# State-space stage of a three-part kernel: regrouping the matrix work by tile size

## The chip, the cores and the metric

The kernel runs on one core of a Trainium2 chip. The metric is the device time of one execution in microseconds (us). Engines go by the names of the profile: PE is TensorE (matmuls), PEld its weight loads, DVE is VectorE, ACT is ScalarE, POOL is GpSimd, SP is SyncE, which here only issues DMAs. All arithmetic is in 32-bit floats; the trace shows two PE instructions for each matmul of this type, and one for each transpose.

## What is computed

An image batch of 4 x 128 channels x 64 x 64 goes through three parts, each added to its input: convolutions with a non-local attention; a bidirectional state-space layer on the 4096 tokens of each image; a sigmoid recurrence over the tokens. The change touches only the second. For one direction it computes, with `A` negative and one `dt` for each token and head:

```python
zxbcdt = x @ in_proj
z, xbc, dt = jnp.split(zxbcdt, [D_INNER, D_INNER + CONV_DIM], axis=-1)
xbc = jax.nn.silu(conv)                      # 4 taps along the tokens
xh, Bm, Cm = jnp.split(xbc, [D_INNER, D_INNER + D_STATE], axis=-1)
...
Lmat = jnp.exp(_segsum(dAc.transpose(0, 1, 3, 2)))      # lower triangle, 0 elsewhere
Y_diag = jnp.einsum('bcln,bcsn,bchls,bcshp->bclhp', Cc, Bc, Lmat, xc)
states = jnp.einsum('bcln,bclh,bclhp->bchpn', Bc, decay_st, xc)
...
Y_off = jnp.einsum('bcln,bchpn,bclh->bclhp', Cc, prev, jnp.exp(Acs))
...
yg = y.reshape(b, l, D_INNER) * jax.nn.silu(z)
yn = yg * jax.lax.rsqrt(jnp.mean(yg * yg, -1, keepdims=True) + EPS) * norm_w
return yn @ out_proj
```

`_segsum` takes the differences of cumulated decays of two tokens of a chunk, and minus infinity where the second token is later. There are 4 heads of 64 channels, a state of 64, and both directions are summed. The result does not depend on the chunk length; the kernel uses 128.

## The kernel before

`mamba` (from L894) walks through 128 steps, 32 for each of the 4 images; a step is one chunk of 128 tokens in both directions. Four steps make a group of 512 tokens; `j` is the step within its group, `G` the group. The loop (L1415 to L1486) works on step n, prepares step n + 1 and loads step n + 2, and between these it does a part of the group's work for the next group (projections) and the last one (outputs), chosen by `j`.

A step's own work on PE, in its order, with the part of the array that each matmul uses (rows x columns):

- `states` (L1212): two products of `bt` and `xdtd` (128x64) into `p_st`. VectorE then adds them to the carried state S (L1230), which GpSimd has multiplied by the chunk's decay (L1227).
- `turn` (L1176): four transposes (128x128) of the next step's x into one PSUM bank.
- `scan` (L1233): eight products of `xdt` and `lt` (128x64, L1240) into `y`; then eight of the carried state S and `ct` (64x64, L1248).
- `prepare` (L1188), for the next step: one transpose of B into `p_bt` (128x128, L1193), two products of B and C into `p_g` (64x128, L1195). ScalarE takes the exponential of the whole of `lt` (L1197) and copies `p_bt` to `bt` (L1199). VectorE multiplies x by dt and dtd (L1202), `p_g` by a triangle of ones (`gm`, L1206), and `lt` by `gm` (L1207). GpSimd multiplies `ct` by C (L1208).

`p_g`, `p_bt` and `p_st` are parts of one PSUM tile, `small`, of two banks.

`lt` [128, 2 directions, 4 heads, 128] starts as a DMA (`load`, L1159) that spreads the row of cumulated decays over all partitions; it has three buffers. `differences` (L1169), at the end of step n for step n + 2, makes it relu(cs - row) on ScalarE, eight instructions with a bias for each partition; Relu keeps the exponent of the part that the triangle will cut from growing. `ct` is loaded in the same way and has two buffers.

The group's work by `j`, the PE part first: j=0 squares of the last group (ScalarE), `project` (L1124), `project_bc` (L1099), `project`; j=1 `means` (L1284, 128x32), `project`, `project_bc`; j=2 `project_fwd` (L1116), `activate`, four `project_z` (L1147), `gate` on GpSimd; j=3 `gate`, and the outputs of the last group in `back` (L1347). `project`, `project_fwd`, `project_z` and `outputs` use the whole array (128x128), `project_bc` uses 128x64, with the two directions in the two halves of the columns. All these take their PSUM tiles from `ring`, which has three banks. From step 4 of an image on, one piece of the next image's opening (`open_sequence`: statistics by transposes, then the scaled input, then the decays) is done at the end of each step, and at every odd step from 5 a piece of the closing statistics of the image before (`ended`).

PE and ScalarE run in the order in which the program is written (`manual_schedule`). VectorE, GpSimd and the DMA queue of SP are put into an order by the framework's planner, by program order and its own estimate of when things are ready[...].

## Time and profile before

| what | value |
|---|---|
| time, median of three runs | 3100.1 us (3091.95 to 3103.64) |
| the profiled execution | 3095.44 us, its span 3093.7 us |
| granted TensorE clock, mean | 0.973 |
| first part (convolution, attention) | to about 1640 us |
| state-space stage | about 1640 to 2960 us |
| busy in 1660 to 2920 us: PE / ACT / DVE / POOL | 1188 / 1019 / 887 / 724 us of 1260 |
| `lt` load, issue to landing | 5.5 us, 512 KB, 128 times |
| ScalarE table loads in lines L1197, L1113, L1122 | 88, 63 and 31 times, 1.28 us each |

The span runs from the first to the last instruction; the time of an execution has 1.7 us more around it. Matmuls are pipelined: the profile's busy time of one is longer than the distance to the next, so PE's cost is best read from start to start in the timeline. In a line of the timeline the first number is the start, the second the length, then engine, line, operation, output <- inputs, for a matmul the rows*columns of the array that it uses, and the shape. What stands in brackets at the end of a line is idle time before it and what ended it. In the list of waits the numbers are the sum in us, how often and the longest; in a group's row they are busy time and the mean of one in ns, then idle time before it.

### The profile page before, as it was taken

The page shows a single profiled execution, that of the slowest core. Times are in us where ns is not written, and L with a number is a line of the kernel's source. Part 1 is how long each engine was busy: PE and PEld are TensorE (multiplying, and loading weights), DVE is VectorE, ACT ScalarE, POOL GpSimd, SP SyncE. Part 2 cuts the span into 40 slices and gives each one's busy share as a digit, 9 for nine tenths or more (in the row PEclk, how much of TensorE's full clock was granted, in tenths as well). Part 3 has the DMA queues.
Part 4 walks back from the last instruction along what each step waited for, and adds up shares of the span by engine and source line. Part 5 has one row for each costly group of instructions (what it writes and reads, how often), then busy time and mean ns, then how long its engine had stood idle before and what let it go on. Part 6 is the DMA issues. An engine that isn't in the chain of part 4 may idle for free. (4 is left out here: it accounts for less than half of the span.)

```text
span 3093.7 us, 51126 instructions
## 1 busy us (share of the span) xinstructions
PE 2858.4 (92%) x19607; PEld 1461.9 (47%) x19607; DVE 2245.6 (73%) x3461; ACT 1834.4 (59%) x3134; POOL 1812.9 (59%) x1393
## 2 busy tenths in 40 slices
PE   6799999999999999999997999998999999999886
PEld 2345444454444554444463444444544444555455
DVE  6886677777787767788865767676777767676667
ACT  3253445444454444444526878876888778888756
POOL 4167458557585575876652565566556565555644
PEclk9899999999999999999998999999999999999988
DMA  5310011010100101011023343433333343333332
GB/s 185 136 39 31 24 47 34 21 44 24 47 32 23 44 24 47 28 50 44 16 81 92 90 124 86 109 88 113 96 96 92 91 103 97 100 102 101 83 111 111
DMA packets 108426, 224.68 MB, mean 73 GB/s; under 512 B 25678, under 2 KB 29390, under 8 KB 106764
## 3 DMA queue, kind: packets, MB, share of 16 engines
q1 hardware_dynamic: 96588, 177.53, 19.8%
q10 hardware_dynamic: 11584, 43.78, 4.2%
q8 instruction: 157, 2.57, 0.4%
q14 instruction: 97, 0.79, 0.1%
HBM read 200.83 MB, written 20.44 MB: 72 GB/s over the span
## 5 line engine op out<-in xcount | busy, mean ns | idle before, releaser
L480 DVE TENSOR_TENSOR es<-es,ex 128x1024 f32<-128x1024 f32 x448 | 703.0, 1569 | 83.6 <-ACT ex L463 43.2
L463 ACT ACTIVATE ex<-pf 128x1024 f32<-128x1024 f32 x512 | 497.8, 1021 | 403.8 <-PE pf L461 365.0
L461 PE MATMUL pf<-theta,phi 64*64 64x512 f32 x4096 | 496.7, 599 | 19.2 <-ACT ex L463 18.8
L473 PE MATMUL acc<-ex,gT 64*64 64x512 f32 x4096 | 486.7, 596 | 7.9 <-ACT ex L463 7.9
L1208 POOL TENSOR_TENSOR ct<-ct,Cst 128x512 f32<-128x512 f32 x128 | 170.0, 1328 | 344.0 <-DMA ct<-csmem 304.8
L1174 ACT ACTIVATE lt<-lt,cs 128x128 f32<-128x128 f32 x1024 | 312.1, 390 | 0.4 <-DMA lt<-csmem 0.4
L367 PE MATMUL pm<-yf,wt 128*128 128x256 f32 x1152 | 287.6, 382 | 15.9 <-DVE es L486 11.5
L473 PEld LDWEIGHTS acc<-ex,gT 64*64 64x64 f32 x4096 | 158.5, 135 | 298.2 <-issue 286.5
L461 PEld LDWEIGHTS pf<-theta,phi 64*64 64x64 f32 x4096 | 147.3, 133 | 311.7 <-issue 212.7
L367 PEld LDWEIGHTS pm<-yf,wt 128*128 128x128 f32 x1152 | 212.6, 189 | 99.2 <-issue 43.5
L410 ACT ACTIVATE eo<-pm 128x256 f32<-128x256 f32 x88 | 33.8, 384 | 367.6 <-PE pm L367 367.6
L1109 PE MATMUL pb<-tl,wbc_fwd 128*64 128x512 f32 x512 | 240.9, 614 | 6.9 <-DVE xT L1141 6.9
L1109 PE MATMUL pb<-tl,wbc_bwd 128*64 128x512 f32 x512 | 241.5, 615 | 0.0
L337 POOL TENSOR_TENSOR yf<-yd 128x272 f32<-128x272 f32 x192 | 230.4, 1228 | 1.4
L1273 POOL TENSOR_TENSOR yT<-yT,zT 128x512 f32<-128x512 f32 x127 | 170.9, 1351 | 57.2 <-DVE yT L1260 49.9
L1207 DVE TENSOR_TENSOR lt<-lt,gm 128x1024 f32<-128x1024 f32 x128 | 178.3, 1393 | 1.9
L337 POOL TENSOR_TENSOR yf<-xp 128x272 f32<-128x272 f32 x128 | 119.0, 961 | 97.4 <-PE pm L367 91.6
L1141 DVE SCALAR_TENSOR_TENSOR xT<-px,taps_bwd,xT 128x512 f32<-128x512 f32 x192 | 143.6, 748 | 9.7 <-ACT xT L1135 5.1
L1109 PEld LDWEIGHTS pb<-tl,wbc_fwd 128*64 128x64 f32 x512 | 66.6, 140 | 173.9 <-issue 142.1
L1240 PE MATMUL y<-lt,xdt 128*64 128x128 f32 x2048 | 141.2, 280 | 6.9 <-PE ptr L1183 4.2
L367 PE MATMUL pm<-yf,wc 128*128 128x256 f32 x512 | 133.4, 389 | 14.8 <-DVE eo L414 8.2
L1227 POOL TENSOR_TENSOR S<-S,tot 128x256 f32<-128x256 f32 x120 | 89.6, 746 | 96.1 <-PE y L1248 85.2
(299 smaller groups left out, 5714.9 us busy)
## 6 DMA issues: line engine op xcount, KB each, us to landing
lt<-csmem SPq DMA_DIRECT2D x128, 512.0 KB, 5.5
wt<-wd ACTq DMA_DIRECT2D x72, 576.0 KB, 3.7
ct<-csmem SPq DMA_DIRECT2D x256, 128.0 KB, 5.2
rs<-m SPq DMA_DIRECT2D x31, 512.0 KB, 3.7
wd<-t SPq DMA_DIRECT2D x16, 576.0 KB, 2.8
t<-in_x SPq DMA_DIRECT2D x4, 2048.0 KB, 10.7
rows<-after SPq DMA_DIRECT2D x32, 256.0 KB, 5.2
out<-t SPq DMA_DIRECT2D x4, 2048.0 KB, 14.3
```

The source lines that it names most:

```text
L337: nc.gpsimd.tensor_tensor(f[:, kx], at(x), at(y), op)
L367: nc.tensor.matmul(pm[:, e, :], wt, src, start=(i == 0), stop=(i == len(terms) - 1))
L461: nc.tensor.matmul(pf[c, e, :], phi[HALF[e], m, c], th[HALF[e]], start=True, stop=True)
L463: nc.scalar.activation(ex, pf, AF.Exp, scale=scale)
L473: nc.tensor.matmul(acc[r][HALF[e]], gT[HALF[r], 2 * m + e, :], ex[HALF[r], e, :], start=(m == 0), stop=(m == NT // 2 - 1),)
L480: nc.vector.tensor_tensor(es, es, ex, ALU.add)
L1109: nc.tensor.matmul(out, w[i]["bc"][:, tap, bass.ts(c, DS)], src, start=(tap == 0), stop=(tap == KC - 1),)
L1141: nc.vector.scalar_tensor_tensor(at(n), px, taps[:, PAD - n : KC - n], at(n), ALU.mult, ALU.add)
L1174: nc.scalar.activation(v, v, AF.Relu, scale=-1.0, bias=m["b"]["cs"][:, d, m["i"], h : h + 1])
L1207: nc.vector.tensor_tensor(lt, lt, gm.unsqueeze(2).to_broadcast([P, ND, NHEAD, P]), ALU.mult)
L1208: nc.gpsimd.tensor_tensor(m["ct"], m["ct"], Cs[:, cols].unsqueeze(1).to_broadcast([P, NHEAD, P]), ALU.mult)
L1273: eng.tensor_tensor(v, v, gr["z"][d][:, :, half(d, j // 2)], ALU.mult)
```

## The change

Five things are changed together.

1. Tile sizes. Products that used 128 columns of the array are issued as two products of 64 columns each (`product`), so `project`, `project_fwd`, `project_z` and `outputs` become 128x64; `means` goes from 128x32 to 128x64; the `p_g` products go from 64x128 to 64x64 (`likeness`). Transposes stay 128x128.
2. Order in a step. `scan` is split into `scan` (products with `lt`) and `carried` (products with S). The new order is `states`, `scan`, `turn` (which now includes the transpose of B), `tokens`, `carried`, `likeness`, `weigh`, then the group's work. `prepare` is dissolved: `tokens` has the copy of `p_bt` and the products with dt and dtd, `weigh` the products of `lt` and of `ct`. Pieces of the opening at steps 4 to 11 of an image, and all of the closing statistics, move from the end of the step to the place between `tokens` and `carried`.
3. Decays. The row and cs are stored negated. GpSimd writes 1e30 into the part of `lt` that the triangle would cut (`mask`, two selects a step), at the start of step n for step n + 2. At the end of step n ScalarE takes exp(bias - lt) in eight instructions (`decays`), instead of Relu there and one exponential in the next step. `gm` and the triangle product are gone; `lt` is multiplied by `p_g` from PSUM.
4. Buffers. `small` becomes two tiles of one bank: the first holds `p_g` of direction 0 and `p_bt`, the second `p_g` of direction 1 and `p_st`. `ct` has three buffers.
5. VectorE is added to the engines that run in program order.

```diff
-        engines = (mybir.EngineType.PE, mybir.EngineType.Activation)
+        engines = (mybir.EngineType.PE, mybir.EngineType.Activation, mybir.EngineType.DVE)
...
-        small = ps.tile([P, 2, NC], F32, name="small")
-        p_g, p_bt, p_st = small[:, :, 0:P], small[:, 0, P : 2 * P], small[:, 1, P : P + DI]
+        small = [ps.tile([P, NC], F32, name=f"small{d}") for d in range(ND)]
+        p_g, p_bt, p_st = [v[:, 0:P] for v in small], small[0][:, P : 2 * P], small[1][:, P : P + DI]
+
+        def product(out, w, src, start=True, stop=True):
+
+            for half in HALF:
+                nc.tensor.matmul(out[half], w[:, half], src, start=start, stop=stop)
...
-            nc.vector.tensor_copy(flat(cs), pcs[:, 0])
+            nc.vector.tensor_scalar(flat(cs), pcs[:, 0], -1.0, None, ALU.mult)
...
-            nc.scalar.activation(row[:, 1], pr, AF.Exp)
+            nc.scalar.activation(row[:, 1], pr, AF.Exp, scale=-1.0)
...
-            nc.tensor.matmul(px, wx, tl[:, rows(g, i, PAD)], start=True, stop=True)
+            product(px, wx, tl[:, rows(g, i, PAD)])
...
-            m["ct"] = wk.tile([P, NHEAD, P], F32, tag="ct", name="ct")
+            m["ct"] = wk.tile([P, NHEAD, P], F32, tag="ct", name="ct", bufs=3)
...
-        def differences(m):
+        def mask(m):
+
+            for d, step in enumerate((-1, 1)):
+                v = m["lt"][:, d]
+                nc.gpsimd.affine_select(
+                    out=v, in_=v, compare_op=ALU.is_ge, fill=1e30, base=0,
+                    pattern=[[0, NHEAD], [-step, P]], channel_multiplier=step,
+                )
+
+        def decays(m):
 
             for d in range(ND):
                 for h in range(NHEAD):
                     v = m["lt"][:, d, h, :]
-                    nc.scalar.activation(v, v, AF.Relu, scale=-1.0, bias=m["b"]["cs"][:, d, m["i"], h : h + 1])
+                    nc.scalar.activation(v, v, AF.Exp, scale=-1.0, bias=m["b"]["cs"][:, d, m["i"], h : h + 1])
...
+            nc.tensor.transpose(p_bt, gr["bc"][0][:, bass.ts(i % MT, P)], k.ident)
+
+        def likeness(m):
+
+            Bs, Cs = (m["g"]["bc"][c] for c in range(2))
+            at = m["i"] % MT * P
+            for h in range(2):
+                for d in range(ND):
+                    nc.tensor.matmul(
+                        p_g[d][HALF[h]], Bs[HALF[d], ds(at + h * DS, DS)], Cs[HALF[d], ds(at, P)],
+                        start=True, stop=True,
+                    )
+
+        def tokens(m):
+
             m["bt"] = wk.tile([P, P], F32, tag="bt", name="bt")
             nc.scalar.copy(m["bt"], p_bt)
...
-            gm = wk.tile([P, ND, P], F32, tag="gm", name="gm")
-            nc.vector.tensor_tensor(gm, p_g, k.tri, ALU.mult)
-            nc.vector.tensor_tensor(lt, lt, gm.unsqueeze(2).to_broadcast([P, ND, NHEAD, P]), ALU.mult)
...
+        def weigh(m):
+
+            for d in range(ND):
+                v = m["lt"][:, d]
+                nc.vector.tensor_tensor(v, v, p_g[d].unsqueeze(1).to_broadcast([P, NHEAD, P]), ALU.mult)
+            Cs = m["g"]["bc"][1][:, bass.ts(m["i"] % MT, P)]
+            nc.gpsimd.tensor_tensor(m["ct"], m["ct"], Cs.unsqueeze(1).to_broadcast([P, NHEAD, P]), ALU.mult)
...
             if n + 2 < N:
                 open_step(n + 2)
+                mask(m[n + 2])
             if n % NT == 0:
                 S = None
             S1 = states(m[n], S)
+            if n % 2 == 0:
+                y = ps.tile([P, ND, 2, 2 * P], F32, tag="y", name="y")
+            scan(m[n], y, S)
...
             if n + 1 < N:
                 turn(m[n + 1])
-            if n % 2 == 0:
-                y = ps.tile([P, ND, 2, 2 * P], F32, tag="y", name="y")
-            scan(m.pop(n), y, S)
+                tokens(m[n + 1])
+            turns = 4 <= at < 4 + NT // GT
+            if turns:
+                run(islice(opening, 1))
+            if at >= 5 and at % 2:
+                run(islice(ending, 1))
...
+            carried(m.pop(n), y, S)
             S = S1
             if n + 1 < N:
-                prepare(m[n + 1])
+                likeness(m[n + 1])
+                weigh(m[n + 1])
...
             if n + 2 < N:
-                differences(m[n + 2])
-
...
+                decays(m[n + 2])
+
+            if at >= 4 and not turns:
                 run(islice(opening, 1))
```

More of the change, by code (lines that the diff above doesn't have):

```diff
@@ L940, in mamba @@
         nc.gpsimd.memset(wdt, 0.0)
-        mean = wp.tile([P, QT], F32, name="mean")
+        mean = wp.tile([P, HD], F32, name="mean")
         nc.gpsimd.memset(mean, 0.0)
@@ L1084, in steps @@
             yield
-            pr = p_g if b == 0 else ring.tile([P, ND, P], F32, tag="big", name="pr")
+            pr = ring.tile([P, ND, P], F32, tag="big", name="pr")
             for i in range(ND):
@@ L1120, in project_fwd @@
             for tap in range(KC):
-                nc.tensor.matmul(px, w[0]["x"][:, tap, :], tl[:, rows(g, 0, tap)], start=(tap == 0), stop=(tap == KC - 1))
+                product(px, w[0]["x"][:, tap, :], tl[:, rows(g, 0, tap)], tap == 0, tap == KC - 1)
             nc.scalar.activation(gr["x"][0][:, 0, :], px, AF.Silu, bias=w[0]["cb"][:, 0:1])
@@ L1151, in project_z @@
             pz = ring.tile([P, MG], F32, tag="big", name="pz")
-            nc.tensor.matmul(pz, w[i]["z"][:, bass.ts(c, P)], tl[:, rows(g, i, PAD)], start=True, stop=True)
+            product(pz, w[i]["z"][:, bass.ts(c, P)], tl[:, rows(g, i, PAD)])
             nc.scalar.activation(gr["z"][i][:, c, :], pz, AF.Silu)
@@ L1186, in turn @@
                     )
-        def prepare(m):
-            gr, i = m["g"], m["i"]
-            Bs, Cs = gr["bc"][0], gr["bc"][1]
-            cols = bass.ts(i % MT, P)
-            nc.tensor.transpose(p_bt, Bs[:, cols], k.ident)
-            for d in range(ND):
-                nc.tensor.matmul(p_g[:, d, :], Bs[HALF[d], cols], Cs[HALF[d], cols], start=True, stop=True)
-            lt = m["lt"]
-            nc.scalar.activation(lt, lt, AF.Exp, scale=-1.0)
+            nc.tensor.transpose(p_bt, gr["bc"][0][:, bass.ts(i % MT, P)], k.ident)
[9 more added lines that the diff above has]
+        def tokens(m):
             m["bt"] = wk.tile([P, P], F32, tag="bt", name="bt")
@@ L1202, in prepare @@
                 nc.vector.tensor_tensor(
-                    m[name], m["xh"], m["b"][name][:, :, i, :].unsqueeze(3).to_broadcast([P, ND, NHEAD, HD]), ALU.mult
+                    m[name], m["xh"], m["b"][name][:, :, m["i"], :].unsqueeze(3).to_broadcast([P, ND, NHEAD, HD]), ALU.mult
                 )
-            gm = wk.tile([P, ND, P], F32, tag="gm", name="gm")
-            nc.vector.tensor_tensor(gm, p_g, k.tri, ALU.mult)
-            nc.vector.tensor_tensor(lt, lt, gm.unsqueeze(2).to_broadcast([P, ND, NHEAD, P]), ALU.mult)
-            nc.gpsimd.tensor_tensor(
-                m["ct"], m["ct"], Cs[:, cols].unsqueeze(1).to_broadcast([P, NHEAD, P]), ALU.mult
-            )
+        def weigh(m):
[4 more added lines that the diff above has]
+            nc.gpsimd.tensor_tensor(m["ct"], m["ct"], Cs.unsqueeze(1).to_broadcast([P, NHEAD, P]), ALU.mult)
         def states(m, S):
@@ L1235, in scan @@
             i = m["i"]
-            at = [bass.ts(i % 2, P), bass.ts(1 - i % 2, P)]
+            at = m["at"] = [bass.ts(i % 2, P), bass.ts(1 - i % 2, P)]
             for c in range(2):
@@ L1243, in scan, with carried @@
                         )
+        def carried(m, y, S):
+            at = m["at"]
             if S is not None:
@@ L1284, in means @@
         def means(gr):
-            pm = ring.tile([ND * QT, MG], F32, tag="big", name="pm")
+            pm = ring.tile([P, MG], F32, tag="big", name="pm")
             for d in range(ND):
-                nc.tensor.matmul(
-                    pm[bass.ts(d, QT)], mean, gr["z"][d][:, 0, :], start=True, stop=True, tile_position=(0, d * QT)
-                )
-            ms = wk.tile([ND * QT, MG], F32, tag="row", name="ms", bufs=3)
+                nc.tensor.matmul(pm[HALF[d]], mean, gr["z"][d][:, 0, :], start=True, stop=True)
+            ms = wk.tile([P, MG], F32, tag="row", name="ms", bufs=3)
             nc.vector.tensor_scalar(ms, pm, RMS_EPS, None, ALU.add)
@@ L1295, in means @@
             m1 = dram.tile([P, n], F32, tag="m1", name="m1")
-            nc.sync.dma_start(m1.rearrange("(d q) n -> d (q n)", d=ND), ms[::QT])
+            nc.sync.dma_start(m1.rearrange("(d q) n -> d (q n)", d=ND), ms[::HD])
             col = wk.tile([P, n], F32, tag="col", name="col")
@@ L1313, in outputs @@
                 for c in range(2):
-                    nc.tensor.matmul(
-                        po[:, half(d, i)], w[d]["out"][:, c, :], gr["y"][d][i][:, c, :],
-                        start=(c == 0), stop=(c == 1),
-                    )
+                    product(po[:, half(d, i)], w[d]["out"][:, c, :], gr["y"][d][i][:, c, :], c == 0, c == 1)
             return po
@@ L1407, in mamba @@
             project(groups[0], i, c)
-        differences(m[0])
+        mask(m[0])
+        decays(m[0])
         for i, c in STEPS_X:
@@ L1411, in mamba @@
         turn(m[0])
-        prepare(m[0])
-        differences(m[1])
+        tokens(m[0])
+        likeness(m[0])
+        weigh(m[0])
+        mask(m[1])
+        decays(m[1])
         S, y = None, None
@@ L1424, in mamba @@
             S1 = states(m[n], S)
+            if n % 2 == 0:
+                y = ps.tile([P, ND, 2, 2 * P], F32, tag="y", name="y")
+            scan(m[n], y, S)
+            at = n % NT
+            if at == 4:
+                opening = open_sequence(b + 1) if b + 1 < B else iter(())
+            if at == 5:
+                ending = ended(b - 1) if after is not None and b > 0 else iter(())
             if n + 1 < N:
                 turn(m[n + 1])
-            if n % 2 == 0:
-                y = ps.tile([P, ND, 2, 2 * P], F32, tag="y", name="y")
-            scan(m.pop(n), y, S)
+                tokens(m[n + 1])
[4 more added lines that the diff above has]
+                run(islice(ending, 1))
+            if mr is not None and b == B - 1 and at in (24, 25, 28, 29):
+                if at == 24:
+                    own = row_statistics(nc, k, ring, "big", wk, t[:, b * T :], mr, (3, 4, 2, 5, 1, 6))
+                next(own)
+            carried(m.pop(n), y, S)
             S = S1
             if n + 1 < N:
-                prepare(m[n + 1])
+                likeness(m[n + 1])
+                weigh(m[n + 1])
             if n % 2:
@@ L1470, in mamba @@
             if n + 2 < N:
-                differences(m[n + 2])
-            i = n % NT
-            if i == 4:
-                opening = open_sequence(b + 1) if b + 1 < B else iter(())
-            if i >= 4:
-                run(islice(opening, 1))
-            if i == 5:
-                ending = ended(b - 1) if after is not None and b > 0 else iter(())
-            if i >= 5 and i % 2:
-                run(islice(ending, 1))
-            if mr is not None and b == B - 1 and i in (24, 25, 28, 29):
-                if i == 24:
-                    own = row_statistics(nc, k, ring, "big", wk, t[:, b * T :], mr, (3, 4, 2, 5, 1, 6))
-                next(own)
+                decays(m[n + 2])
+            if at >= 4 and not turns:
+                run(islice(opening, 1))
         squares(gr, (1,), True)
```

## The prediction

> **What bounds the kernel now.** I read the page first, then busy time by stretches, then the timeline of single steps, and the list of waits last.

> ```profile
> PE 2858.4 (92%) x19607; PEld 1461.9 (47%) x19607; DVE 2245.6 (73%) x3461; ACT 1834.4 (59%) x3134; POOL 1812.9 (59%) x1393
> ```
> ```profile
> 1660.00:2920.00 1260.00, 1188.18 (x8208) 610.59 (x8208) 887.43 (x1937) 1019.34 (x2023) 723.91 (x601) 0.98 0.37 99
> ```

> The second line is the state-space stage, the only one that the change touches: 1260 us for 31.5 groups of four steps, 40.0 us a group. Its columns are PE, PEld, DVE, ACT, POOL. PE is busy 94% of it, ACT 81, DVE 70, POOL 57. So PE bounds the stage, and the question is what PE spends. One step (j=1 into j=2, timeline of PE):

> ```profile
> 2296.96 0.61 PE L1218 MATMUL small<-xdtd,bt 128*64 128x256 f32 x4
> 2297.50 0.66 PE L1183 MATMUL ptr<-ident,xT 128*128 128x128 f32 x4
> 2298.09 1.09 PE L1240 MATMUL y<-lt,xdt 128*64 128x128 f32 x16
> 2299.11 0.67 PE L1248 MATMUL y<-ct,S 64*64 64x128 f32 x16
> 2299.71 0.33 PE L1193 MATMUL small<-ident,Bst 128*128 128x128 f32 x1
> 2299.97 0.49 PE L1195 MATMUL small<-Cst,Bst 64*128 64x128 f32 x4
> 2300.39 3.70 PE L1121 MATMUL px<-tl,wx_fwd 128*128 128x512 f32 x8
> ```

> The first number is the start in us, 128*64 and the like the tile size (rows*columns of the array in use). Every line has another tile size than the line above. From start to start these runs take 0.58 (0.54 here, behind a run of its own size), 0.59, 1.02, 0.60, 0.26 and 0.42 us. Inside a run a 512-column instruction follows the last after 0.43 us, a 128-column one after 0.11; across a change of size it is 0.52 and 0.20. A change costs 0.09 us, and 0.05 to 0.1 more in the first weights of the new run. The trace gives the sum directly: pb (L1109) alone takes 3.59 us to the next run, L1218 0.58; where they follow each other in one size they take 3.49 + 0.54. **Joining two runs saves 0.15 us.**

> **The sum for PE.** Before, a group is 4 x 3.47 (the six runs) = 13.9, plus the group's work: j=0 px 1.06 + pb 3.59 + px 1.06; j=1 pm 0.98 + px 1.06 + pb 3.44; j=2 7.58; j=3 3.65. Total 36.3 us without waits. The group from 2278.5 to 2314.4 took 35.9 (it lacks one L1218), so the sum holds. The sequence's own PE work (statistics, steps) is some 46 us in the stage, or 1.5 a group; 40.0 - 36.3 - 1.5 leaves 2.2 us a group of waits (71 us).

> After, a step has three runs: states and scan (0.58 + 1.02 - 0.15 = 1.45), five transposes (0.59 + 0.11 = 0.70), and carried with likeness, now both 64*64 (0.60 + two waves of 0.11 = 0.81): 2.96, x4 = 11.85. All the group's work is 128*64, the size in which the next states start: 12 waves of 0.427 in j=0 and in j=1 (5.12 each), j=2 16 waves and the 0.57 that it now waits for its PSUM ring (7.4), j=3 16 of 0.214 and some start (3.5). Total 33.0. Of 31 changes of size in a group 12 stay. **Saved 3.3 us a group, 105 us over 32 groups.**

> [...] Both halves of `product` use all 128 rows[...]. The trace shows pb, the same shape: two loads side by side, and a pair of 512-column matmuls each 0.43 us, as long as one whole 128*128. I take the row: nothing.

> **The added wait.** p_g and p_bt shared the tile `small`; now p_g[0] and p_bt share small0, p_g[1] and p_st share small1. The copy of p_bt (ACT, L1199) stood behind the p_g matmuls; in `tokens` it stands ahead of them. The list of waits says what that means:

> ```profile
> DVE gm L1206 <- ACT bt L1199: 58.5, 42, 2.8
> PEld small L1193 <- DVE S L1230: 31.9, 32, 4.5
> ```

> gm reads p_g and waits for a copy that reads p_bt, other columns of the tile; L1193 writes p_bt and waits for a reader of p_st. So the program orders accesses to such a tile whether the columns meet or not, and likeness will wait for the copy. The copy is in ACT's queue behind the last step's decays. ACT in the same step now:

> ```profile
> 2297.18 0.69 ACT L1113 ACTIVATE Cst<-pb,bc_bias 128x512 f32<-128x512 f32 x1 [1.53 <-PE pb L1109]
> 2297.76 2.43 ACT L1174 ACTIVATE lt<-lt,cs 128x128 f32<-128x128 f32 x8
> 2300.21 1.28 ACT L1197 ACT_TABLE_LOAD   x1
> 2301.51 1.06 ACT L1197 ACTIVATE lt<-lt 128x1024 f32<-128x1024 f32 x1
> 2302.47 0.25 ACT L1199 COPY bt<-small 128x128 f32<-128x128 f32 x1
> ```

> The chain starts 0.2 us after PE enters the step (Silu of pb's end), and the copy ends 5.8 after it; today that hurts nobody. After: Silu 0.70, table load 1.28, eight Exp, copy 0.25. Exp with a bias of its own is not in the trace at this shape; the Relu of the same operands is 390 ns and the Sigmoid with bias 395 (L1589), so I keep 2.4 for eight. The copy ends at 0.2 + 0.7 + 1.3 + 2.4 + 0.25 = 4.85. PE could start likeness at 1.45 + 0.70 + 0.50 (carried) = 2.65: **it stalls 2.2 us.** From j=0 the chain starts with px's Identity (0.78), from j=2 with the last Silu of z (0.60): 2.2 and 2.1. After j=3 there is no Silu and no load, and ACT is ahead. Sum 6.5 us a group. Behind likeness, PE's whole queue waits: all projections and the next states; the chain starts anew from their end, so the stall repeats. [...] In the lines above the load starts 0.02 us after the last Relu and the Exp 0.02 after the load: I take 1.28.

> **The other parts.** VectorE: gm (416 ns) and the 128x1024 product (1393) go, two 128x512 products with one operand in PSUM come; the nearest row is xdt (684): 1.37 for 1.81, beside PE, worth nothing. Program order puts S's add behind the three taps of the last px in j=1: 0.2 + 0.78 + 0.24 + 2.3 + 0.4 = 3.9 us after entry, later than 2.65 but before the copy: covered by that stall, 1.3 us a group (41 us) if the cover is gone. Behind S's add are tokens and weigh; scan needs weigh by the next step, 5 us on: free.

> GpSimd: two selects of 128x512 a step. Nearest rows:

> ```profile
> L390 POOL COPY t<-eo 128x512 f32<-128x512 f32 x4 | 2.6, 660 | 55.8 <-DVE eo L418 55.8
> L48 POOL TENSOR_SCALAR_AFFINE_SELECT tri<-tri 128x128 f32<-128x128 f32 x2 | 0.6, 302 | 0.0
> masks.py:383 POOL TENSOR_SCALAR_AFFINE_SELECT gmean<-gmean 128x128 f32<-128x128 f32 x1 | 0.5, 536 | 0.0
> ```

> Between 0.66 (a copy) and 4 x 0.302 = 1.21. With 0.1 fixed (the memsets) and 7.5 ns a row (the third line has 32 rows): 0.1 + 4 x 0.2 + 0.02 = 0.93. So 7.4 us a group on POOL's 23.0: 30.4 of 40, hidden on average. lt's load moves too: SP issues it when scan is done, and scan now comes before the transposes, 0.7 us sooner; it lands after 5.6, and mask has to be done only by the end of the next step. ct's third buffer lets its load go a step earlier; what it ends is POOL's wait for ct (304.8 us), off the path: nothing. The negated cs, the wider `mean` and pr's new buffer act once a group or a sequence on instructions of the same size: nothing. The pieces of the next sequence that move into the transposes fall into the stall: some 44 of 0.44 us, -19 us. The ring waits of pb behind VectorE's taps (about 1 us a group) are swallowed by the stall; the rest of the old waits, 1.1 us, I keep, S's in j=0 above all.

> **Sum.** Before 40.0 a group. After 33.0 + 1.5 + 6.5 + 1.1 - 0.6 = 41.5: +1.5, times 32 = +48 us. On the profiled execution (span 3093.7, 3095.4 with what lies around it) that is 3143; the median of the runs, 3100.1, is 4.7 higher. I forecast **3145 us**, own range 3095 to 3195 (copy 0.5 us sooner or later three times a group: 48 us each way).

> **Rivals.** (1) Likeness is not held (the tiles' order is finer than I read it, or ACT is ahead): then -105, +41 from S's add, -25 of ring waits: about 3010. It decides if the copy ends before 3.7 us, 1.1 sooner in each of three steps; against it is that gm waits for the copy in 42 steps. (2) POOL becomes serial: a mask that stands in the queue before its load has landed holds S's product, ct and the gates. Today's waits for ct, 9.7 us a group, moved to mask make 30.4 + 9.7 + 2.7 (its waits for PE) = 42.8 a group, over 1.3 more than mine: 3185 to 3230. It decides once mask and its wait pass 4 us a step; lt's early load speaks against it. (3) Gain and stall cancel: the old waits vanish too, 3095 to 3110. That sizes stay unjoined is no rival: only wdt and rs_t keep a fourth, some 30 runs.

> **Chances.** A measurement tells 0.5% (15 us) from no change. Forecast 0.54, of which 0.42 slower and 0.12 within; rival 1 0.24; rival 2 0.18; rival 3 0.02 beyond that, and 0.02 for the unforeseen, slower. Faster 0.24, same 0.14, slower 0.62. The range takes in half of rival 1 and most of rival 2: 3005 to 3220.

> **What would show it.** Right: PE idle before likeness released by ACT bt, near 2 us in three steps of four; runs as summed; POOL near 75%; exp loads as many as now. Wrong: no idle there and a group near 35 us; or idle at decays for POOL's mask; or weigh late at scan.

## The result, and the profile after

The changed kernel takes **3240.4 us** (median of four runs, 3231.3 to 3244.0), beside 3096.0 for the kernel before: ratio 1.046, 95% interval 1.0426 to 1.0494. The forecast was 3145, its range ended at 3220: slower as forecast, but by 144 us instead of 49. The profiled execution spans 3238.2 us, 144.5 more. Until 1640 us the two traces are alike and the last part is too; all of it lies in the state-space stage.

First the engines' row and the groups of the changed lines on the page (busy us, mean ns | idle before them), then the stage in the windows view (columns as in the prediction, then granted clock):

```profile
PE 2829.7 (87%) x21335; PEld 1440.5 (44%) x21335; DVE 2250.8 (70%) x3461; ACT 1716.6 (53%) x3008; POOL 1901.0 (59%) x1649
...
L1178 POOL TENSOR_SCALAR_AFFINE_SELECT lt<-lt 128x512 f32<-128x512 f32 x256 | 157.5, 637 | 358.5 <-DMA lt<-csmem 301.9
L1188 ACT ACTIVATE lt<-lt,cs 128x128 f32<-128x128 f32 x1024 | 313.0, 388 | 1.1
...
L1209 PE MATMUL small<-Cst,Bst 64*64 64x128 f32 x1024 | 70.2, 309 | 204.2 <-ACT bt L1217 169.5
...
L1228 DVE TENSOR_TENSOR lt<-lt,small 128x512 f32<-128x512 f32 x256 | 163.9, 681 | 79.4 <-ACT bt L1217 59.7
```
```profile
1660.00:3064.00 1404.00, 1161.66 (x9876) 592.30 (x9873) 890.47 (x1940) 905.36 (x1901) 815.25 (x858) 0.93 0.35 90
```

The prices came out: a mask 637 ns (taken: 930; the copy of the same size, at 660, was nearer), an Exp with bias 388 (taken: the Relu's 390), a product 681 (684). ScalarE has 114 us less work than before, VectorE the same, GpSimd 91 more, which makes it 58% busy where the prediction had near 75. PE is busy 83% of its stage instead of 94%. The list of waits of the stage names the place:

```profile
POOL lt L1178 <- DMA lt<-csmem: 301.9, 82, 8.4
...
PE small L1209 <- ACT bt L1217: 169.5, 96, 3.9
...
PE small L1209 <- DVE S L1250: 34.4, 13, 5.0
```

`likeness` waits for the copy of `p_bt` 96 times, three steps of four, as forecast. Two sums over short slices lead further: **idle and clock**. I cut the stage into slices of 1 us (windows view) and added up, for every kernel, PE's busy time, the time at half clock (twice the sum of 1 minus the granted clock) and what that costs while PE is busy (busy time by 1 minus the clock).

| us in the stage | before | after | difference |
|---|---|---|---|
| PE busy, of it lost to the clock | 1188, 21 | 1162, 73 | -26, +52 |
| PE busy at full clock | 1168 | 1089 | -79 |
| PE idle | 72 | 242 | +170 |
| at half clock | 48 | 185 | +137 |
| length of the stage | 1260 | 1404 | +144 |

The forecast had -105 for the matrix work, +153 for waits (7.0 us a group instead of 2.2, times 32) and nothing for the clock. So -105, +153, 0 stand against -79, +170, +52. Matmul ends are modelled in the profile, so how a difference divides between busy and idle is less sure than their sum; the granted clock is on record as it is. One regular stall, in the timeline of PE:

```profile
2427.12 0.67 PE L1272 MATMUL y<-ct,S 64*64 64x128 f32 x16
2429.79 0.55 PE L1209 MATMUL small<-Cst,Bst 64*64 64x128 f32 x8 [2.00 <-ACT bt L1217]
2430.26 3.49 PE L1003 MATMUL po<-yT,wout_fwd 128*64 128x256 f32 x16
2433.58 1.89 PE L1003 MATMUL po<-yT,wout_bwd 128*64 128x256 f32 x16
```

The last two lines are the same sixteen matmuls for the two directions: 3.49 us behind the stall, 1.89 after. The granted clock of these microseconds, third number from the right:

```profile
2429.00:2430.00 1.00, 0.21 (x8) 0.21 (x8) 0.00 (x0) 1.00 (x6) 0.00 (x0) 1.00 0.66 174
2430.00:2431.00 1.00, 1.00 (x12) 0.53 (x6) 0.58 (x1) 1.00 (x5) 0.00 (x0) 0.51 0.91 264
...
2432.00:2433.00 1.00, 1.00 (x8) 0.60 (x6) 0.71 (x2) 0.08 (x1) 1.00 (x2) 0.50 0.00 0
...
2434.00:2435.00 1.00, 1.00 (x12) 0.68 (x10) 0.34 (x1) 0.00 (x0) 1.00 (x2) 1.00 0.00 0
```

Such a stall is paid twice: while it lasts, and by 3.4 us at half speed behind it. But not every one is: in the stage 43 idle stretches of PE last 1.9 to 2.5 us, and 23 of them are followed by a drop within 2.5 us.

```profile
2426.60:2430.01 3.41, 1.41 (x29) 0.98 (x28) 1.29 (x2) 3.40 (x12) 1.19 (x2) 1.00 0.49 114
2430.01:2433.42 3.41, 3.41 (x24) 1.83 (x18) 2.16 (x4) 2.07 (x8) 1.53 (x3) 0.50 0.41 117
2433.42:2436.84 3.42, 3.42 (x41) 2.41 (x38) 2.18 (x5) 0.00 (x0) 3.33 (x3) 1.00 0.00 0
```
```profile
2071.61:2075.03 3.42, 1.74 (x30) 1.16 (x25) 1.40 (x3) 3.41 (x9) 1.74 (x2) 1.00 0.39 93
2075.03:2078.44 3.41, 3.09 (x34) 2.05 (x36) 2.07 (x4) 2.62 (x10) 0.45 (x1) 1.00 0.64 142
```

PE is busy 41% of the first window, and the next one runs at half clock; in the second case it is 51 and 91%, and the clock stays. Of the stage's windows at full clock, 34 of the 36 in which PE was busy less than half are followed by a slow one, and 1 of the 321 others. The 43 stalls divide cleanly: in the 23 with a drop PE was busy at most 48% of the worse of the two windows, in the 20 without at least 49%.

Where the regular steps' stalls are as forecast, some steps of each image are far longer. Here is step 25 of the second image (DVE, ACT and PE lines of the timeline):

```profile
2312.00 2.33 DVE L1146 SCALAR_TENSOR_TENSOR xT<-px,taps_fwd,xT 128x512 f32<-128x512 f32 x3
...
2314.79 1.28 ACT L1052 ACT_TABLE_LOAD   x1
2316.08 0.42 ACT L1052 ACTIVATE xe<-u 128x256 f32<-128x256 f32 x1
2316.40 0.25 ACT L1217 COPY bt<-small 128x128 f32<-128x128 f32 x1
2316.53 1.75 DVE L1053 RECIPROCAL u<-u 128x256 f32<-128x256 f32 x1 [2.21 <-ACT xe L1052]
...
2319.81 0.49 DVE L1060 TENSOR_TENSOR xe<-dt,A 128x128 f32<-128x128 f32 x2
2320.22 0.41 DVE L1250 TENSOR_TENSOR S<-S,small 128x256 f32<-128x256 f32 x1
...
2320.69 0.70 PE L1209 MATMUL small<-Cst,Bst 64*64 64x128 f32 x6 [3.56 <-DVE S L1250]
```

A piece of the next image's opening (L1048 to L1060) stands in VectorE's program order ahead of the add of S, behind the taps; it waits for a logarithm on ScalarE, and everything behind it waits too. The second tile of `likeness` cannot start before that add has read `p_st`. And the logarithm with its table load stands ahead of the copy.

### The profile page after: what moved, and what is told of

It reads as the page before. It is cut to its first block, busy times and chain, and to the rows that moved or that the text cites. A ratio compares the mean times of both kernels' runs of the same rounds, so it can differ in the third digit from the quotient of the medians.

```text
span 3238.2 us, 55107 instructions
## 1 busy us (share of the span) xinstructions
PE 2829.7 (87%) x21335; PEld 1440.5 (44%) x21335; DVE 2250.8 (70%) x3461; ACT 1716.6 (53%) x3008; POOL 1901.0 (59%) x1649
## 5 line engine op out<-in xcount | busy, mean ns | idle before, releaser
L1178 POOL TENSOR_SCALAR_AFFINE_SELECT lt<-lt 128x512 f32<-128x512 f32 x256 | 157.5, 637 | 358.5 <-DMA lt<-csmem 301.9
L1209 PE MATMUL small<-Cst,Bst 64*64 64x128 f32 x1024 | 70.2, 309 | 204.2 <-ACT bt L1217 169.5
L1230 POOL TENSOR_TENSOR ct<-ct,Cst 128x512 f32<-128x512 f32 x128 | 162.9, 1274 | 105.7 <-ACT Cst L1118 92.8
L1228 DVE TENSOR_TENSOR lt<-lt,small 128x512 f32<-128x512 f32 x256 | 163.9, 681 | 79.4 <-ACT bt L1217 59.7
L1297 POOL TENSOR_TENSOR yT<-yT,zT 128x512 f32<-128x512 f32 x127 | 160.8, 1278 | 37.8 <-ACT zT L1158 36.7
L1250 DVE TENSOR_TENSOR S<-S,small 128x256 f32<-128x256 f32 x120 | 49.7, 414 | 175.7 <-PE small L1238 157.9
L1146 DVE SCALAR_TENSOR_TENSOR xT<-px,taps_bwd,xT 128x512 f32<-128x512 f32 x192 | 144.3, 751 | 21.1 <-ACT xT L1140 10.4
L1220 DVE TENSOR_TENSOR xdt<-ptr,dt 128x512 f32<-128x512 f32 x128 | 88.0, 688 | 85.4 <-PE ptr L1197 85.3
```

Source lines behind the costliest of these rows:

```text
L1178: nc.gpsimd.affine_select(out=v, in_=v, compare_op=ALU.is_ge, fill=1e30, base=0, pattern=[[0, NHEAD], [-step, P]], channel_multiplier=step,)
L1228: nc.vector.tensor_tensor(v, v, p_g[d].unsqueeze(1).to_broadcast([P, NHEAD, P]), ALU.mult)
L1230: nc.gpsimd.tensor_tensor(m["ct"], m["ct"], Cs.unsqueeze(1).to_broadcast([P, NHEAD, P]), ALU.mult)
L1297: eng.tensor_tensor(v, v, gr["z"][d][:, :, half(d, j // 2)], ALU.mult)
```

## The experiments

My theory after the result: the stall is there as priced, and the rest comes from VectorE's program order in the irregular steps. Rivals: GpSimd's masks, and (later) the clock. Ratios are against runs of the kernel before on the same chip.

### The copy, and the order on VectorE

```diff
@@ copy late: in tokens, and as keep(m) behind likeness
-            nc.scalar.copy(m["bt"], p_bt)
...
                 likeness(m[n + 1])
+                keep(m[n + 1])
@@ planned
-        engines = (mybir.EngineType.PE, mybir.EngineType.Activation, mybir.EngineType.DVE)
+        engines = (mybir.EngineType.PE, mybir.EngineType.Activation)
```

Copy late alone:

> The changed kernel with one move: the copy of p_bt stands behind likeness instead of ahead of it, in the program's order; all else as changed. Theory A (likeness is held by the copy, which is behind the decays in ScalarE's queue): PE's idle time before likeness that the copy ends goes from 170 to below 15 us. What is late next is S's add behind the last px's three taps, about 1.2 us in one step of four, 40 us. The time falls by 140 to 200 us, to 3040 to 3100. Theory B (VectorE's program order is what costs; the copy only happens to be last): the wait moves to S's add or to weigh and the time falls by less than 40 us. Theory C (GpSimd's masks hold the decays): less than 40 us too, with idle time on ScalarE ahead of the decays.

VectorE planned alone:

> The changed kernel with VectorE's order left to the planner again, one word of the diff undone. Theory A: the regular step keeps its 2.2 us stall before likeness in three of four; only the steps in which a piece of the next image's opening stands ahead of S's add (steps 13, 16, 17, 21, 24, 25 of an image, some 85 us over the changed kernel's regular steps) get shorter: 3150 to 3190. Theory B: below 3110. If the order costs nothing: 3240, within 15.

Both:

> Both: the copy behind likeness, VectorE planned. Theory A: the two costs add, and the sum of the joined runs shows: 33.0 us of PE a group, 1.5 of sequence work, 1 to 2 of waits, so 36 to 37 a group against 40.0 before: 2970 to 3010. If the joined runs save nothing and the stall was all there was: about 3095.

Measured: copy late **3184.7** (1.0281, 1.0259 to 1.0303), planned **3201.0** (1.0353, 1.0324 to 1.0382), both **3115.8** (1.0074, 1.0049 to 1.0100). All three expectations missed, to the slow side. 56 and 39 us alone make 125 together: each covers the other. With the copy gone, PE waits for the add of S in its place (waits of the stage, copy late, then both):

```profile
PE small L1209 <- DVE S L1253: 112.2, 40, 14.4
```
```profile
PE small L1209 <- DVE S L1253: 25.2, 15, 5.2
```

So the copy alone is not the loss, and the two together leave the kernel still 20 us above the one before. The sums of the stage with both say why: at full clock PE is busy 75 us less than before, but it is idle 74 us more, and the clock costs 10 more. Of the 146 us of idle time 63 now end with VectorE's taps, which still read a PSUM bank that PE wants (12 before); in the waits, for instance:

```profile
PE ls_in L83 <- DVE xT L1146: 24.7, 13, 9.8
PE pm L1316 <- DVE xT L1146: 16.3, 4, 7.2
```

### Order and tile sizes, each alone on the kernel before

> The kernel before, with VectorE added to the engines that run in program order and nothing else. Theory A (program order costs by itself: the add of S stands behind the taps of the last px and behind the opening's small instructions, whatever the order of the step on PE): 3125 to 3155 us. Theory B (program order costs only together with the copy ahead of likeness and the late gates, since in the old step PE needs S only after the transposes and eight products of scan, 2 us later): within 15 us of the kernel before, 3080 to 3110 us. I hold A a little likelier: putting VectorE back under the planner gained 39 us alone and 69 us together with the moved copy.

> The kernel before, with only the tile sizes of the group's work changed (128 columns issued as two halves of 64, means 64 wide); order of the step, decays, buffers and VectorE as before. Theory A (a join of two runs of one size saves 0.15 us, a half costs nothing extra): about 9 joins a group, 1.35 us times 32 = 43 us, so 3045 to 3065 us. [...] Theory C (the planner's order of VectorE and the waits eat it): 3080 to 3100 us.

```diff
@@ in order
-        engines = (mybir.EngineType.PE, mybir.EngineType.Activation)
+        engines = (mybir.EngineType.PE, mybir.EngineType.Activation, mybir.EngineType.DVE)
@@ halves: project, project_fwd, project_z, outputs; means 64 wide
-            nc.tensor.matmul(px, wx, tl[:, rows(g, i, PAD)], start=True, stop=True)
+            product(px, wx, tl[:, rows(g, i, PAD)])
```

One word in a list costs **118 us**: 3214.6, ratio 1.0389 (1.0360 to 1.0417). That is more than any theory had. The waits of the stage, and the step of the kind shown above:

```profile
PE small L1193 <- DVE S L1230: 103.7, 53, 6.2
```
```profile
2280.02 1.22 DVE L1043 TENSOR_SCALAR u<-xe 128x256 f32<-128x256 f32 x1
2281.27 1.23 DVE L1044 TENSOR_SCALAR u<-u 128x256 f32<-128x256 f32 x1
2282.54 1.37 DVE L1045 TENSOR_TENSOR u<-xe,u 128x256 f32<-128x256 f32 x1
2283.82 0.41 DVE L1230 TENSOR_TENSOR S<-S,small 128x256 f32<-128x256 f32 x1
...
2284.29 0.47 PE L1193 MATMUL small<-ident,Bst 128*128 128x128 f32 x1 [3.25 <-DVE S L1230]
```

The wait for S was 23.3 us before. By place: 31 of the 32 steps j=1, which follow j=0, wait for S, 1.8 us at the median; behind the taps alone PE waits 22 times, 35 us in all, nearly all of it there. Most of the other 69 us stand behind pieces of the opening and the closing, as in the lines above, 29 of them in steps j=0; after j=1 PE hardly waits for S (6 us in six steps). Steps 24 to 26 of an image lose 37 us together. In the sums: idle +78, clock +42.

The halves give **3085.7**, ratio 0.9960 (0.9945 to 0.9974): faster, but 11 us where 43 were expected. The halves themselves cost what the prediction took from pb: in the trace after, the two pairs of px (L1003) take 0.86 us from start to start (2216.84 to 2217.70), 0.43 a pair. In the medians j=0 gains 0.56 us a step and j=2 0.23, and j=1 loses 0.39, for a wait that was 6.9 us before:

```profile
PE pb L1114 <- DVE xT L1146: 18.2, 20, 2.3
```

My reading is that px is done sooner, so `pb` comes sooner to the bank that VectorE's taps still read. A shorter run of matmuls is worth nothing where its end is not what the next run waits for.

### The irregular steps: pieces, scalings, masks

> The kernel after, with one thing moved: all pieces of the next image's opening, not only those of steps 4 to 11, are issued between tokens and carried, so that on VectorE they stand behind the add of S instead of ahead of it. Theory A (the unpriced part of the slowdown is the add of S held behind these pieces in program order, seen at steps 24 and 25 of an image): 25 to 45 us less than the kernel after, 3195 to 3215 us. Theory B (the pieces only show the loss there, PE would wait for the copy of p_bt as long): within 15 us of it, 3225 to 3255 us.

> The kernel after, with the eight scalings of the next image's input (128x512 each, four images) computed mostly by VectorE, also for later images, instead of by GpSimd. Theory A (GpSimd's unbroken batch of them holds the product of S, the gates and, at its end, VectorE's own instruction with two operands in SBUF; seen at steps 16 and 17): 25 to 45 us less than the kernel after, 3195 to 3215 us, and no VectorE instruction of 128x3 above 2 us. Theory B (VectorE in program order pays the same for them): within 15 us, 3225 to 3255 us.

> The changed kernel without the two selects of GpSimd in each step; the decays take a constant bias of one column in place of cs, in the same instructions, so that the unmasked numbers stay finite (the masking and the differences are left out). Theory A: the masks are hidden; the time stays within 25 us of 3240. Theory C (GpSimd is a serial link: its 8.5 us batch of the next image's scaling and the masks hold S's product): it falls by 60 us or more.

```diff
@@ pieces behind the add of S
-            turns = 4 <= at < 4 + NT // GT
+            turns = at >= 4
@@ scalings
-                eng = nc.vector if b == 0 and j % 3 < 2 else nc.gpsimd
+                eng = nc.vector if b or j % 3 < 2 else nc.gpsimd
@@ no mask: the two selects gone, one constant bias for all decays
-        mask(m[0])
...
-                    nc.scalar.activation(v, v, AF.Exp, scale=-1.0, bias=m["b"]["cs"][:, d, m["i"], h : h + 1])
+                    nc.scalar.activation(v, v, AF.Exp, scale=-1.0, bias=k.neghalf)
```

Pieces **3184.9** (1.0289, 1.0258 to 1.0319): 55 us less than after, more than expected; the wait for S falls from 34.4 to 1.0 us, that for the copy stays (162.6). Since the move also changes the pieces' place on PE and ScalarE, not all of the 55 need be VectorE's order; under the planner the same move gains 25 (below). Scalings **3223.8** (1.0404, 1.0373 to 1.0435): 17 less, between the two theories, for steps 20 get 9 us longer in exchange. Masks left out **3219.3** (1.0403, 1.0380 to 1.0425): 21 less, inside the band that said masks are not the main loss. These gains overlap at steps 16 and 17, so they are not to be added.

### Both, with the order kept; and the taps moved too

> The kernel after, with the copy of p_bt behind likeness and all pieces of the next image's opening behind tokens; VectorE still in program order, GpSimd's masks kept. Theory A (program order is the larger cost and what is left of it are the three taps of the last px ahead of the add of S, 1.4 us at the step after j=0 and 2.1 us after j=1 as in the old kernel in that order): the two gains add up, 55 + 55 us, 3120 to 3140 us, with PE's waits before likeness ended by the add of S, some 60 to 110 us of them. Theory B (with copy and pieces out of the way the step runs at the sum of the matrix work): 3000 to 3050 us.

> As the kernel with copy and pieces moved, and the taps of the second px of j=0 and of the px of j=1 issued in the next step behind tokens, so that nothing of the group's work stands ahead of the add of S on VectorE. Theory A (VectorE's program order, taps ahead of S, is what was left): 60 to 110 us less than the run without this, 3010 to 3070 us, and faster than the kernel before. Theory B (S is late because its product on GpSimd or ScalarE's queue is late, not because of the taps): within 25 us of the run without it.

```diff
@@ taps behind: project(..., later=taps) for two of the three px
-            for n in range(1, KC):
+            rest() if later is None else later.append(rest)
...
                 tokens(m[n + 1])
+            run(f() for f in taps)
```

Copy and pieces: **3111.2** (1.0046, 1.0023 to 1.0068), a gain of 129 where the two alone make 111, with 56.9 us of waits for S left, near what theory A had; 55 of them stand in steps after j=0, not after j=1. Moving the taps then made it **slower**, 3131.6 (1.0109, 1.0077 to 1.0141). That is inside theory B's band, but not for its reason: the wait for S falls to 9, and another appears, for the PSUM bank that px holds until its late taps:

```profile
PE pm L1320 <- DVE xT L1148: 33.3, 8, 6.2
PE px L1003 <- DVE xT L1148: 24.7, 12, 4.4
```

The reading (S behind the taps) was right, the cure moved the wait: in each of these two fixed orders one of the two is late. The planner is not free of it either: with copy late and pieces behind (next section) PE waits 10 us for S and 57 behind the taps.

### What the masks cost once the rest is gone

> The kernel after, with the copy of p_bt behind likeness, VectorE given back to the planner, and all pieces of the opening behind tokens. Theory A (the pieces cost because program order sets them ahead of the add of S; under the planner that no longer holds): within 20 us of the same kernel without moved pieces, so 3095 to 3135 us. Theory B (the pieces cost by their place on PE and ScalarE, whoever orders VectorE): 35 to 60 us less than it, 3055 to 3080 us.

> The kernel after, with the copy of p_bt behind likeness, VectorE given back to the planner, and the decays as in the kernel before (Relu at the end of the step, one Exp of the whole lt in the next, triangle and gm on VectorE), so that GpSimd has no mask; tile sizes, order of the step and buffers as after. Theory A (the masks, which stand in GpSimd's queue until their load has landed and hold the product of S, ct and the gates behind them, are what keeps that version from the sum of the matrix work): 60 to 100 us less than with masks, 3015 to 3055 us, faster than the kernel before. Theory B (the masks cost the 20 us that leaving them out gave in the kernel after): 3085 to 3105 us.

> The kernel after, with the copy of p_bt behind likeness, VectorE given back to the planner, the decays as in the kernel before (no masks) and all pieces of the opening behind tokens. Theory A (masks and pieces are two losses): the gains of 40 and 25 us add up, 3040 to 3060 us. Theory B (both are one loss, GpSimd's queue at the steps with pieces): within 10 us of the version that has only the decays as before, 3065 to 3085 us.

> The kernel after, with the copy of p_bt behind likeness, VectorE given back to the planner, all pieces of the opening behind tokens, and the masks issued at the end of the step, straight ahead of the decays that read them, instead of at its start. Theory A (the masks cost by waiting for their load at the head of GpSimd's queue): 25 to 45 us less than with the masks at the start, 3045 to 3065 us, and GpSimd's wait for the load of lt under 80 us. Theory B (they cost by their work, 5 us a group, or the planner puts them at the same place): within 15 us, 3075 to 3105 us.

```diff
@@ Relu back: no mask; in tokens
+            nc.scalar.activation(m["lt"], m["lt"], AF.Exp, scale=-1.0)
@@ in weigh
+                nc.vector.tensor_tensor(gm[:, d], p_g[d], k.tri[:, d], ALU.mult)
@@ mask last
             if n + 2 < N:
+                mask(m[n + 2])
                 decays(m[n + 2])
```

All four have the copy late and VectorE planned. Pieces behind: **3090.5** (0.9983, 0.9966 to 0.9999), between the two theories, 25 us below the same kernel without. Decays as before: **3075.0** (0.9915, 0.9885 to 0.9946), 41 less, again between its theories. Both: **3064.3** (0.9903, 0.9885 to 0.9921), at the edge of theory B: with the masks gone the pieces' place is worth 11, not 25. Mask last: **3083.2** (0.9957, 0.9941 to 0.9972), nothing settled, since GpSimd's wait for their load did not move (230.1 us without the change):

```profile
POOL lt L1178 <- DMA lt<-csmem: 232.5, 74, 6.0
```

Whether the masks cost by their work or by that wait stays open, and the 41 us are those of the whole of part 3 of the change, which also moves ScalarE's and VectorE's work. The version with the decays as before and the pieces behind **beats both kernels**, by 32 and 176 us. Its stage:

```profile
1660.00:2886.00 1226.00, 1094.18 (x9846) 591.68 (x9847) 902.37 (x2057) 1016.57 (x2016) 703.49 (x602) 0.97 0.39 101
```

At full clock PE is busy 1061 us of it, 107 less than before: the whole of the 105 that was forecast. Idle is still 132 us; 57 of it lies before `scan` with no releaser that the profile names. By the timeline, 26 of these 27 waits end 0.10 us after VectorE's last product that reads `y` (L1290): `scan` now comes early in the step and, as I read it, waits for a tile that VectorE still reads.

### The clock: cause or company?

> The kernel after, with 12 products of a zero weight (128x64) and the identity added to y behind carried, in the three steps of a group in which PE stalls 2.2 us before likeness: some 1.5 us of work for PE in each, 96 times, which changes no value and releases nobody earlier. Theory A (a stall of about 2 us makes the chip halve TensorE's clock for some 3.4 us, and this is a part of the loss that was not priced): the time at half clock falls from 185 us to under 100, and the kernel gets 20 to 50 us faster than after, 3190 to 3220 us, though it does more. Theory B (the low clock only accompanies the stalls, or the filling itself delays likeness): the same time as after or up to 30 us slower, 3235 to 3270 us.

> As the kernel with 12 products of zero, with 16 of them, some 2.0 us of work a stall. Theory A: within 15 us of it, since the rest of the stall is 0.2 us either way and the clock stays up in both; a few us slower if the filling begins to reach past the end of the stall. Theory B: slower than after by more than with 12.

```diff
             carried(m[n], y, S)
+            if j:
+                fill(m[n], y)
@@ fill: 12 (16) times
+                nc.tensor.matmul(
+                    y[HALF[h], d, c, m["at"][d]], zero, k.ident, start=False, stop=True, skip_group_check=True
+                )
```

Twelve products of zero: **3211.7** (1.0374, 1.0351 to 1.0396), 29 us less than after, with 576 more matmul instructions an image that release nobody sooner. Half clock falls from 185 to 92 us, its cost from 73 to 30; windows in which PE is busy less than half, from 36 to 14. The filling and what is left of the stall, in its timeline and its waits:

```profile
1846.87 1.53 PE L1283 MATMUL y<-ident,zero 128*64 128x128 f32 x24
```
```profile
PE small L1211 <- ACT bt L1219: 42.6, 68, 2.5
```

Sixteen: 3228.0 (1.0416, 1.0396 to 1.0437), 16 more than with twelve and past theory A's few us: 2.0 us of filling reaches past the end of many stalls (the wait for the copy is down to 18 us in 40 steps), and the half clock does not fall further (113 us). The clock is a cause: more work in the stall made the kernel faster.

## Why the prediction was wrong

**The failed step** is the price of the stall, "**it stalls 2.2 us**" and the sum built on it, 6.5 us a group, at a clock taken as unchanged. The length was right: from start to start, in steps that PE enters at full clock, the stall is 2.36, 2.26 and 2.18 us, 6.8 a group. (Where a slow stretch has made PE late it is shorter, so that PE's waits for the copy sum to 169.5 us, 5.3 a group.) What the sum put at nothing is the clock behind the stalls: +52 us, more than half of the 95 that are missing; the rest is 26 of matrix work and 17 of idle time. Of the 73 us that the clock costs after the change, 41 follow a wait of 1.9 to 2.5 us, 26 one of over 3.4 us in the irregular steps. The table before showed a mean clock of 0.973, and no step asked what made it less than 1.

**Program order on VectorE** was priced at 41 us "if the cover is gone" and nothing otherwise. On the kernel before it costs 118. The term itself had the right place and size (35 us behind the taps alone). Left out were the pieces of the opening and the closing that stand ahead of S too, and again the clock, 42 us. Of the pieces the prediction said that they "fall into the stall: some 44 of 0.44 us, -19 us"; those that stayed at the end of a step do the opposite, and setting all of them behind the add gained 55. The cover did hold in the regular steps.

**The matrix work.** Runs without waits cost what was summed, 33 us a group; in PE's busy time at full clock the gain is 79 of the 105 forecast (107 in the fastest version), of which the modelled ends can hide a part. Alone, in the old order, joined runs gave a quarter of their sum.

**Masks**: 637 ns for 930, no bound of the stage (GpSimd 58% busy), yet leaving them out gained 21 us, and going back to the old decays 41 without the other losses, where the sum had nothing. The wait that rival 2 named is there (a mask at the head of GpSimd's queue, its load not landed, 301.9 us), but not at its price, and whether it is what the masks cost is open. **Rival 1**, likeness not held, was built: 3116 with the planner, 3185 in program order, not 3010. A table load costs its own 1.28 us and nothing behind it that shows: in step 25 it ends 0.01 us before the logarithm starts.

## What to carry to other kernels

Price a stall of the matmul engine twice: its length, and the half-speed stretch that may follow; in these traces it follows when PE is busy less than about half of one 3.41 us window. Read the granted clock around the stalls that are there already. When an engine is put into program order, list for each instruction that PE waits for all that now stands ahead of it, in every kind of step and not only in the regular one. A wait removed shows what stood behind it, so test two suspected waits alone and together.

## What the runs showed of the hardware

**The clock.** In the traces before and after, the granted clock is 1.00 or 0.50 and nothing between, and a slow stretch of the stage is one to four windows of 3.41 us. The length of an idle stretch alone does not decide: of those of 1.9 to 2.5 us, 23 of 43 were followed by a drop. What counts here is the share of a window. Over the state-space stage of all 18 traces, a window at full clock was followed by a slow one in 230 of 232 cases where PE was busy under 40% of it, in 165 of 381 between 40 and 58%, and in 1 of 5687 above. And after a slow window the clock stayed low in all 193 cases where PE was busy under 80% of that window, in 28 of 415 above. These shares rest on the modelled ends of matmuls.

**VectorE held by GpSimd.** Four additions of 128x3 with both inputs in SBUF took 6.55 to 6.57 us each, where the median is 0.26. One of them:

```profile
2216.16 6.55 DVE L1144 TENSOR_TENSOR xT<-xT,xT 128x3 f32<-128x3 f32 x1 [4.36 <-ACT xT L1140]
2217.22 0.61 POOL L1247 TENSOR_TENSOR S<-S,tot 128x256 f32<-128x256 f32 x1
2217.79 2.50 POOL L1306 TENSOR_TENSOR zT<-zT 128x512 f32<-128x512 f32 x2
...
2220.23 1.22 POOL L1178 TENSOR_SCALAR_AFFINE_SELECT lt<-lt 128x512 f32<-128x512 f32 x2
2221.42 1.27 POOL L1230 TENSOR_TENSOR ct<-ct,Cst 128x512 f32<-128x512 f32 x1
```

It ends 0.02 us after the last of an unbroken row of GpSimd instructions. Without the two masks in that row it took 5.37, and with the scalings moved no such addition took over 2.9. Instructions with one input in PSUM show nothing of the kind in this trace: the 288 taps of L1146 took 749 to 755 ns, with GpSimd busy at the start of 152 of them, and the 256 products of L1228 took 669 to 690, with GpSimd busy at the start of 92. That a VectorE instruction with both inputs in SBUF can be held for a whole row of GpSimd's is how I read these lines; no run has it alone.
